# A patch-code convolution block on one core: the softmax numerators of a quad moved one slot behind its logits, with four buffers for the exponentials

## The chip, the cores and the metric

The kernel runs on one core of one Trainium2 chip. The metric is the device time of one execution in microseconds (us). Executions of one kernel on one chip differ by up to 0.6% here, so every kernel is compared through runs of the kernel before on the same chip. A run counts as slow when it is over 1.5% above the fastest of the same kernel.

## The reference, cut to what matters

The block normalises x over groups of channels, then applies two layers. Each layer takes the 3x3 patches p of every channel, weighs that channel's 16 centroids by a softmax of the negative squared distance, and replaces the patch by the weighted centroid before an ordinary multiplication with the weights. A batch norm follows each layer, a ReLU the first, a gate and the residuals the second.

```python
# x: (16, 256, 28, 28) float32; centroids (256, 16, 9); w_sub (256, 9, 256)
def amm_conv3x3(x, centroids, w_sub):
    p = patches(x)                                   # (B, 784, C, 9)
    d = |p|^2 - 2 p.centroids + |centroids|^2        # (B, 784, C, 16)
    attn = softmax(-d)
    lut = einsum('cks,cso->cko', centroids, w_sub)
    return einsum('bnck,cko->bno', attn, lut)
# out = relu(bn(amm1(gn(x)))); out = se(bn(amm2(out))); result = x + relu(out + gn(x))
```

## The kernel before

The work is cut into quads: 4 x 4 tiles of 32x32 on TensorE for one part of the channels and 384 or 400 pixels. A tile of pixels has 8 quads, an image two tiles, a layer 16 quads. The kernel lays one quad of the layer into each *slot*, and lists for a slot, in this order, the logits, the exponentials, some *looks* (128-wide matmuls that add finished quads to the output), the numerators, the turning and scaling of the numerators, and the remaining looks. Engines run their lists in order.

```python
ring = [p_ring.tile([P, 2, 512], F32, name=f"pair{i}") for i in range(3)]   # 3 pairs of PSUM banks
...
def logits(u, rows):                       # TensorE, L563: 16 tiles into two pairs
    ps = [pair(), pair()]
    ...
def b_exp(u):                              # ScalarE, L621: one exponential per pair
    for ps in u.pop("lg"):
        e = epool.tile([P, 2, 400], F32, tag="e", name="e")
        nc.scalar.activation(e[:, :, :n], ps[:, :, :n], AF.Exp, scale=2.0)
def b_num(u):                              # TensorE, L631: numerators and sums, again two pairs
    es = u.pop("e")
    u["nm"] = [pair(), pair()]
    ...
def b_turn(u):                             # VectorE: transposes nt (L643), reciprocal rc (L649)
def c_scale(u):                            # GpSimd: k = nt * rc (L659), tails, range check totals
def c_turn(u):                             # VectorE, a slot later: q = transpose of k (L677)
def c_look(u, o, h):                       # TensorE, L695: acc += ws . q
...
LC = 3                                     # looks of a tile begin 3 slots after its logits
LOGITS, LOAD, MOVE, EXP, LOOK_A, NUM, TURN, SMALL, LOOK_B, MAX, LOOK_C, TURN_BACK, REST = range(13)
...
        def norm(self, b, t):              # group norm of the next image
            self.at(t, REST, gn_stats, b, 0)      # VectorE, needs x
            self.at(t + 1, REST, gn_stats, b, 1)
            self.at(t + 2, SMALL, gn_mean, b)     # TensorE, L423
            self.at(t + 3, SMALL, gn_var, b)      # TensorE, L434
            self.at(t + 4, REST, gn_apply, b, 0)
            self.at(t + 5, REST, gn_apply, b, 1)
...
            plan.at(n0 - 2, REST, load_x, b, x[b])
            plan.norm(b, n0)
```

In the second layer two of each tile's quads also get their maxima ahead of time (another logits block, some VectorE work and a small round trip through DRAM), which makes 576 logits blocks and 512 numerator blocks.

Of the kernel before, what the change touches and what calls it, by code (L numbers as in the profile page):

```python
# [23 lines left out]
NQ = NT // 4  # L24
# [45 lines left out]
def kernel(  # L70
# [328 lines left out]
        nc.vector.tensor_add(wd[l], wd[l], mones_sb[:, l].unsqueeze(1).to_broadcast([P, NT, 32]))  # L399

    tpool = ctx.enter_context(tc.tile_pool(name="tpool", bufs=3))
    epool = ctx.enter_context(tc.tile_pool(name="epool", bufs=2))
    npool = ctx.enter_context(tc.tile_pool(name="npool", bufs=2))
    kpool = ctx.enter_context(tc.tile_pool(name="kpool", bufs=3))
    qpool = ctx.enter_context(tc.tile_pool(name="qpool", bufs=3))
# [314 lines left out]
            )  # L720


    LC = 3
    LOOKS = [(m, o, h) for m in range(NQ) for o in range(2) for h in range(3 if m % 4 == 3 else 2)]

    LOGITS, LOAD, MOVE, EXP, LOOK_A, NUM, TURN, SMALL, LOOK_B, MAX, LOOK_C, TURN_BACK, REST = range(13)

    class Plan:
        def __init__(self, step, lead, lb):
            self.step = step  # L730
            self.lead = lead
            self.lb = lb
            self.ns = len(PXT) * NQ * step
            self.end = self.ns + LC * step
            self.jobs = {}
            self.tiles = []
            self.loads = []

        def at(self, slot, pos, f, *a):
            self.jobs.setdefault((slot, pos), []).append((f, a))  # L740

        def emit(self):

            free = [-99] * len(pts)
            for slot, last, u in sorted(self.loads, key=lambda v: v[:2]):
                tile = free.index(min(free))
                assert free[tile] <= slot
                free[tile] = last
                self.at(slot, LOAD, patches, u, tile)
            for n0, of in self.tiles:  # L750

                slots = [n0 + (LC + q) * self.step for q in range(NQ)]
                more = [2 if (s, MAX) in self.jobs else 0 for s in slots]
                k, room = 0, len(LOOKS) - sum(more)
                for q, s in enumerate(slots):
                    n = (q + 1) * room // NQ - q * room // NQ + more[q]
                    for i, (m, o, h) in enumerate(LOOKS[k : k + n]):
                        self.at(s, LOOK_A if i < n // 2 + n % 2 - more[q] // 2 else LOOK_B if i < n - more[q] else LOOK_C, c_look, of[m], o, h)
                    k += n
            for key in sorted(self.jobs):  # L760
                for f, a in self.jobs[key]:
                    f(*a)

        def stage(self, l, b, pat, s0, maxed):
            at = self.at
            for pi, px in enumerate(PXT):
                n0 = s0 + pi * NQ * self.step
                of = []
                for m in range(NQ):
                    s = n0 + m * self.step  # L770
                    u = {"l": l, "b": b, "pi": pi, "px": px, "pat": pat, "key": (l, b, pi), "m": m, "maxed": m in maxed}
                    of.append(u)
                    if m in maxed:
                        a = s - self.lb
                        self.loads.append((a - self.lead, s, u))
                        at(a, MAX, a_logits, u)
                        at(a, MAX, a_turn, u)
                        at(a + 1, TURN_BACK, a_max, u, 0)
                        at(a + 2, TURN_BACK, a_max, u, 1)
                        at(a + 2, TURN_BACK, m_turn, u)  # L780
                        at(a + 3, MOVE, m_out, u)
                        at(a + 4, MOVE, m_in, u)
                    else:
                        self.loads.append((s - self.lead, s, u))
                    at(s, LOGITS, b_logits, u)
                    at(s, EXP, b_exp, u)
                    at(s, NUM, b_num, u)
                    at(s, TURN, b_turn, u)
                    at(s, TURN, c_scale, u)
                    at(s + 1, TURN_BACK, c_turn, u)  # L790
                self.tiles.append((n0, of))

        def prep(self, l, pat, t):
# [42 lines left out]
    def pat_of(l, b):  # L836
        return d_pat[2 * l + b % 2]
# [17 lines left out]
    plan = Plan(1, 3, 6)  # L855
    for si, (l, b) in enumerate(stages):
        t = si * NS
        plan.stage(l, b, pat_of(l, b), t, () if l == 0 else MAXED)
        if l == 0 and b >= 1:
            n0 = -3 if b == 1 else t - 2 * NS - 3  # L860
            plan.at(n0 - 2, REST, load_x, b, x[b])
            plan.norm(b, n0)
            plan.prep(0, pat_of(0, b), {1: 1, 2: 32, 3: 56}.get(b, t - 2 * NS + 3))
        if l == 1:
            if b in (0, B - 1):
                t0 = t - NS + LC
                plan.prep_near(1, pat_of(1, b), t0, 4, t0 + 4, 8)
            else:
                plan.prep(1, pat_of(1, b), 44 if b == 1 else t - 2 * NS + LC + 1)
            plan.at(t + NS, REST, load_x, b, x[b])  # L870
            plan.close(b, out[b], t + NS + LC, 1 if b < B - 2 else 2)
    for i in range(len(STEPS)):
# [36 lines left out]
    with tc.If(flag > 0):  # L909
        with tc.For_i(0, B) as bi:  # L910
            load_x("g", x[bass.ds(bi, 1)].rearrange("o c n -> (o c) n"))
            plan = Plan(8, 3, 6)
# [84 lines left out]
```

## Time and profile before

| | before |
|---|---|
| median of 3 runs | 2970.67 us |
| span of the profiled run | 2969.2 us |
| granted TensorE clock | 0.989 |
| TensorE / VectorE / ScalarE / GpSimd busy | 97 / 76 / 37 / 60% |

The page follows the chain of work that ended last back from the end, and gives its shares of the span, first by engine and then by line (page of the kernel before):

```profile
PE 79%; DMA 7%; DVE 6%; POOL 4%; issue 2%; ACT 2%; SPq 0%; ACTq 0%; DVEq 0%; POOLq 0%
```

The reader is to see that TensorE is on the path for four fifths of the time, and that some transfers and VectorE work, 13% together, stand on it too. ScalarE, which makes the exponentials, seems to play no part: its short waits, spread over hundreds of slots, show only when a slot is looked at by itself. The lines for that are in the prediction.

### The profile page before, as it was taken

What the parts mean: (1) busy time and instruction counts of PE and PEld (TensorE: products, weight loads), DVE (VectorE), ACT (ScalarE), POOL (GpSimd) and SP (SyncE); (2) the same over time, 40 slices, a digit from 0 to 9 for tenths busy, and PEclk for the clock granted to TensorE, in tenths of its full rate; (3) what the DMA queues carried; (4) which work ended last, traced back from release to release, by engine and by line L of the source; (5) the groups of instructions that cost most, each with busy time, mean ns of one, the idle gap of its engine ahead of it and who ended that gap; (6) DMA issues with size and microseconds to landing.
All of it is one profiled execution on the core that took longest, in us unless ns stands there. A gap on an engine that the chain in (4) does not pass through costs nothing.

```text
span 2969.2 us, 94838 instructions
## 1 busy us (share of the span) xinstructions
PE 2871.6 (97%) x39834; PEld 1145.4 (39%) x39834; DVE 2252.7 (76%) x2760; ACT 1092.7 (37%) x1605; POOL 1768.5 (60%) x2583
## 2 busy tenths in 40 slices
PE   4999999999999999999999999999999999999995
PEld 2433333333333333333333333333333333334332
DVE  3476777787877878787787877878788787878884
ACT  1332343433434343343433434343343434333332
POOL 3474575666656566665656656566665656656553
PEclk8999999999999999999999999999999999999998
DMA  6877777767767676776767667676776767674641
GB/s 185 227 174 170 203 219 195 212 154 213 186 169 197 151 208 174 197 185 154 211 156 207 180 180 188 154 214 156 214 185 163 200 155 206 177 189 106 163 114 56
DMA packets 296773, 530.30 MB, mean 179 GB/s; under 512 B 94240, under 2 KB 251664, under 8 KB 296336
## 3 DMA queue, kind: packets, MB, share of 16 engines
q0 software_dynamic: 51648, 269.78, 34.9%
q1 hardware_dynamic: 242512, 251.70, 32.7%
q8 instruction: 316, 5.18, 0.7%
q10 hardware_dynamic: 2176, 2.65, 0.3%
q14 instruction: 121, 0.99, 0.1%
HBM read 269.96 MB, written 254.05 MB: 176 GB/s over the span
## 4 chain that ended last, share of the span: by engine, by line
PE 79%; DMA 7%; DVE 6%; POOL 4%; issue 2%; ACT 2%; SPq 0%; ACTq 0%; DVEq 0%; POOLq 0%
PE acc L695 47%; PE pair L631 16%; PE pair L563 14%; DMA xt<-in_x 4%; DVE nt L643 2%; POOL k L659 2%; DVE rc L649 1%; DVE gn_st L417 1%; POOL total L671 1%; DMA pt<-pat 1%; ACT e L621 1%; DMA ws<-dws 1%; PE pair L309 0%; PE pair L324 0%; DVE q L677 0%
## 5 line engine op out<-in xcount | busy, mean ns | idle before, releaser
L695 PE MATMUL acc<-q,ws 128*128 128x384 f32 (+1 forms) x4096 | 1641.0, 519 | 9.7 <-ACT y L717 9.7
L659 POOL TENSOR_TENSOR k<-nt,rc 128x832 f32<-128x832 f32 (+1 forms) x512 | 802.3, 1567 | 1132.9 <-DVE rc L649 1120.5
L643 DVE STREAM_TRANSPOSE nt<-pair 128x832 f32<-128x832 f32 (+1 forms) x1024 | 976.3, 992 | 603.5 <-PE pair L631 506.4
L621 ACT ACTIVATE e<-pair 128x800 f32<-128x800 f32 (+1 forms) x1024 | 787.8, 821 | 1358.8 <-PE pair L563 1357.3
L695 PEld LDWEIGHTS acc<-q,ws 128*128 128x128 f32 x4096 | 696.9, 189 | 907.7 <-issue 577.2
L631 PE MATMUL pair<-e,cw 32*32 32x384 f32 (+1 forms) x16384 | 580.3, 502 | 11.9 <-ACT e L621 10.6
L563 PE MATMUL pair<-pt,wd 19*32 19x384 f32 (+2 forms) x18432 | 561.0, 500 | 5.9 <-DMA pt<-pat 3.3
L677 DVE STREAM_TRANSPOSE q<-k 128x832 f32<-128x832 f32 (+1 forms) x512 | 489.1, 955 | 0.8 <-POOL k L659 0.8
L649 DVE RECIPROCAL rc<-nt 128x104 f32<-128x104 f32 (+1 forms) x512 | 398.5, 778 | 17.6
L631 PEld LDWEIGHTS pair<-e,cw 32*32 32x32 f32 x16384 | 167.5, 103 | 349.2 <-ACT e L621 321.4
L563 PEld LDWEIGHTS pair<-pt,wd 19*32 19x32 f32 (+1 forms) x18432 | 138.4, 103 | 340.1 <-issue 265.5
L665 POOL TENSOR_TENSOR tail<-nt,rc 128x104 f32<-128x104 f32 (+1 forms) x512 | 242.4, 473 | 0.0
L695 PE MATMUL acc<-qt,ws 128*128 128x400 f32 (+1 forms) x512 | 218.6, 509 | 0.0
L671 POOL TENSOR_TENSOR total<-total,nt 128x96 f32<-128x96 f32 (+1 forms) x448 | 198.7, 443 | 0.0
L468 POOL DMA_DIRECT2D pat<-side x280 | 186.6, 667 | 1.1 <-DMA pat<-im 0.7
L671 POOL TENSOR_TENSOR total<-total,rc 128x96 f32<-128x96 f32 (+1 forms) x448 | 175.5, 392 | 0.0
L695 PEld LDWEIGHTS acc<-qt,ws 128*128 128x128 f32 x512 | 90.8, 189 | 100.1 <-issue 50.6
L587 DVE TENSOR_REDUCE mx<-z 128x48 f32<-128x768 f32 (+1 forms) x128 | 120.8, 943 | 0.0
L582 DVE STREAM_TRANSPOSE z<-pair 128x768 f32<-128x768 f32 (+1 forms) x128 | 119.2, 969 | 0.0
L468 POOL DMA_DIRECT2D pat<-im x140 | 94.0, 672 | 3.5 <-ACT im L447 3.5
L707 ACT ACTIVATE im<-acc,bnsh,bnsc 128x384 f32<-128x384 f32 (+1 forms) x64 | 43.4, 678 | 139.4 <-PE acc L695 133.4
L717 ACT ACTIVATE y<-acc,bnsh,bnsc 128x384 f32<-128x384 f32 (+1 forms) x64 | 43.4, 679 | 91.7 <-PE acc L695 76.8
(106 smaller groups left out, 753.5 us busy)
## 6 DMA issues: line engine op xcount, KB each, us to landing
pat<-side POOLq DMA_DIRECT2D x232, 588.0 KB, 6.1
pt<-pat SPq DMA_DIRECT2D x1024, 112.5 KB
pt<-pat SPq DMA_DIRECT2D x1024, 108.0 KB
pat<-im POOLq DMA_DIRECT2D x116, 588.0 KB, 5.3
xt<-in_x POOLq DMA_DIRECT2D x32, 784.0 KB, 8.8
out_dram<-y POOLq DMA_DIRECT2D x16, 784.0 KB, 4.0
pat<-side POOLq DMA_DIRECT2D x24, 300.0 KB, 6.1
pat<-side POOLq DMA_DIRECT2D x24, 288.0 KB, 6.0
```

Of the source, the lines that this page charges most:

```text
L468: nc.gpsimd.dma_start(view(pat, (ROWS * p0 + 9 * k + 3 * dx) * HW + px, [[ROWS * HW, m], [HW, 3], [1, n]]), bass.AP(v.tensor, v.offset, [l ...
L563: nc.tensor.matmul(ps[t // 2][c : c + 32, t % 2, :n], lhsT=wd[l][32 * i : 32 * i + rows, 4 * u["m"] + t, :], rhs=u["pt"][32 * i : 32 * i + ...
L587: nc.vector.tensor_reduce(u["mx"][:, 2 * v : 2 * v + 2].rearrange("p t (j b) -> p t b j", j=2)[:, :, :nb], u["z"].pop(0)[:, : 64 * nb].rea ...
L621: nc.scalar.activation(e[:, :, :n], ps[:, :, :n], AF.Exp, scale=2.0)
L631: nc.tensor.matmul(u["nm"][t // 2][32 * i : 32 * i + 32, t % 2, :n], lhsT=cw[l][c : c + 32, 4 * u["m"] + t, :], rhs=es[t // 2][c : c + 32, ...
L643: nc.vector.transpose(nt[:, :nb, 2 * v : 2 * v + 2].rearrange("p b t r -> p t b r"), ps[:, :, : 32 * nb].rearrange("p t (b r) -> p t b r", ...
L649: nc.vector.reciprocal(rc[:, : 8 * nb], u["nt"][:, :, SUM])
L659: nc.gpsimd.tensor_tensor(q[:, :nb].rearrange("p b (a s) -> p (b a) s", s=8), nt[:, :, :8], rc.unsqueeze(2).to_broadcast([P, 8 * nb, 8]), ...
L665: nc.gpsimd.tensor_tensor(tails[key][:, :nb, 8 * (m % 4) : 8 * (m % 4) + 8], nt[:, :, 8].rearrange("p (b a) -> p b a", a=8), rc.rearrange( ...
L671: nc.gpsimd.tensor_add(t[:, : 8 * nb], t[:, : 8 * nb], v)
L677: nc.vector.transpose(q[:, :, : 32 * nb].rearrange("p h (b r) -> p h b r", r=32), u.pop("k")[:, :nb].rearrange("p b (h r) -> p h b r", h=2),)
L695: nc.tensor.matmul(accs[key][:, :n], lhsT=ws[l][:, 2 * m + h if h < 2 else 2 * NQ + m // 4, o * P : (o + 1) * P], rhs=u["q"][h][:, :n], st ...
```

## The change

The intent: the numerators of a quad no longer follow the exponentials of that same quad within the slot. They run one slot later, on exponentials that have long been made, while ScalarE works on the new slot's. For that a pair of exponentials must live a slot longer, hence four buffers; everything behind the numerators moves a slot too, hence LC = 4. The patches of the first and the last image are prepared in three slots instead of four before their first use, to make up for the later outputs.

```diff
-    epool = ctx.enter_context(tc.tile_pool(name="epool", bufs=2))
+    epool = ctx.enter_context(tc.tile_pool(name="epool", bufs=4))
...
-    LC = 3
+    LC = 4
...
-            self.end = self.ns + LC * step
+            self.lc = LC if step == 1 else 3
+            self.end = self.ns + self.lc * step
...
-                slots = [n0 + (LC + q) * self.step for q in range(NQ)]
+                slots = [n0 + (self.lc + q) * self.step for q in range(NQ)]
...
-                    at(s, NUM, b_num, u)
-                    at(s, TURN, b_turn, u)
-                    at(s, TURN, c_scale, u)
-                    at(s + 1, TURN_BACK, c_turn, u)
+                    at(s + 1, NUM, b_num, u)
+                    at(s + 1, TURN, b_turn, u)
+                    at(s + 1, TURN, c_scale, u)
+                    at(s + 2, TURN_BACK, c_turn, u)
...
-                plan.prep_near(1, pat_of(1, b), t0, 4, t0 + 4, 8)
+                plan.prep_near(1, pat_of(1, b), t0, 3, t0 + 3, 8)
```

## The prediction

> **What bounds the kernel now.** I read the page's first part, then the list of waits, then the timeline of a quiet stretch, then the busy time by window. The page's first line and three of its costliest groups:
>
> ```profile
> PE 2871.6 (97%) x39834; PEld 1145.4 (39%) x39834; DVE 2252.7 (76%) x2760; ACT 1092.7 (37%) x1605; POOL 1768.5 (60%) x2583
> ...
> L621 ACT ACTIVATE e<-pair 128x800 f32<-128x800 f32 (+1 forms) x1024 | 787.8, 821 | 1358.8 <-PE pair L563 1357.3
> ...
> L631 PE MATMUL pair<-e,cw 32*32 32x384 f32 (+1 forms) x16384 | 580.3, 502 | 11.9 <-ACT e L621 10.6
> L563 PE MATMUL pair<-pt,wd 19*32 19x384 f32 (+2 forms) x18432 | 561.0, 500 | 5.9 <-DMA pt<-pat 3.3
> ```
>
> TensorE carries the path (79% of the chain that ended last), but its 97% hides gaps, because matmuls overlap. The reader is to see that 16,384 numerator matmuls (L631) are charged 580 us and 18,432 logit matmuls (L563), 12% more of them, only 561 us: the numerators stand still somewhere. The list of waits names the suspects (who waited for whom: total us, times, longest):
>
> ```profile
> PEld pair L631 <- ACT e L621: 321.4, 555, 7.1
> PEld acc L695 <- issue: 627.9, 983, 1.3
> ```
>
> Most of the 321 us is no loss: 0.57 us of idle weight load stands before every small-tile block, logits too, and there it is called "issue". What is lost shows in the timeline of one slot of a quiet stretch (start, us, engine, line, count, idle before):
>
> ```profile
> 1516.05 0.93 PE L563 MATMUL pair<-pt,wd 21*32 21x384 f32 x32
> ...
> 1516.91 1.61 PE L695 MATMUL acc<-q,ws 128*128 128x400 f32 x4
> 1517.09 1.51 ACT L621 ACTIVATE e<-pair 128x768 f32<-128x768 f32 x2 [3.47 <-PE pair L563]
> ...
> 1518.45 1.08 PE L631 MATMUL pair<-e,cw 32*32 32x384 f32 x32
> ...
> 1519.47 1.61 PE L695 MATMUL acc<-q,ws 128*128 128x400 f32 x4
> ...
> 1521.01 0.23 PEld L563 LDWEIGHTS pair<-pt,wd 19*32 19x32 f32 x32 [0.57 <-issue]
> 1521.01 0.93 PE L563 MATMUL pair<-pt,wd 19*32 19x384 f32 x32
> ```
>
> A slot is four blocks: logits, 2 looks (L695), numerators, 2 looks; 4.96 us from 1516.05 to 1521.01. The two blocks of 32 small matmuls have the same shape but one takes 1.08 and the other 0.93. The two exponentials end at 1518.60; the numerators begin at 1518.45 with the first pair's, and the second pair's must wait for the second exponential. In the single records of this block the last start lies 0.60 us after the first; in the logits 0.45. So this slot loses 0.15 us, between two halves of one block, and nothing before the block.
>
> **Size of that loss over the whole trace.** For each of the 512 numerator blocks I took the distance from first to last start and subtracted 0.46 us (the undisturbed distance is 0.45 to 0.46). 138 blocks lose nothing (mostly slots with three looks ahead of the numerators, whose two extra 0.34 us matmuls cover the exponentials), 321 lose 0.10 to 0.30, and 42 lose 0.60 to 0.70 (the exponentials stand behind copies and evacuations on ScalarE). Sum: **95.1 us**: 3.8 before 135 us, 2.4 to 230, 1.6 to 282, 2.7 to 380, 80.5 in 380 to 2790, 4.2 after. A second loss is the whole block starting late for the first exponential: 8.3 us in 31 blocks, and once 6.5 us at 78 us.
>
> **What the Trainium skill says.** "Trainium Kernel Development and Optimization", Performance Expectations, says that matmul busy time is a bad metric because matmuls are pipelined; the trace agrees (97% busy beside 95 us of stalls). "TensorE: Matmul & The Clock Gate", Part 3, The mechanism, says matmuls start and end in strict program order; so the waiting half-block holds the looks behind it, and the trace agrees: L695 at 1519.47 follows the last numerator by the same 0.41 us as after logits. "TensorEngine Tiling (Array Packing)", Key Properties: "Mode switching requires drain"; the 627.9 us of "issue" before 128-wide weight loads, about 0.65 us each, look like it. "PSUM — Partial Sum Buffer", its part on bank collisions, asks that a bank be guarded until its reader is done; the ring of three PSUM pairs does that, and it makes the first rival below.
>
> **The change part by part.**
> - *Numerators one slot later.* The two program-order listings of TensorE show the same four blocks a slot, in the same places: logits, looks, numerators, looks. Two looks still lie between logits and numerators, so "next to" removes no change of tile mode: 0 us. What moves is which exponentials the block needs: those of a slot ago, about 4 us old. The listing shows its first half waiting for VectorE alone.
> - *Four exponential buffers.* A pair of exponentials now lives a slot longer; with four, the write of the next finds its buffer freed by the numerators of the slot before. No wait, no cost.
> - *The ring.* The numerators' second half writes the pair from which the first exponential of the same slot reads. In the quiet slot that one (half of 1.51 us from 1517.09) ends near 1517.9, and the second half may start at 1518.5: 0.6 us to spare. So the 95.1 us go, but the late starts (8.3 and 6.5 us) largely stay, now on the second half.
> - *LC 3 to 4.* One more slot of looks at the end, with as much less at the start: I count +2 us, since the start is held by transfers. The early preparation for the first and last image is squeezed from four slots to three, and the first second-layer stage already waits for transfers (11.5 us of stalls in logits blocks between 230 and 282 us): +4 there, +2 for the last image, both my choice.
>
> Gross gain: 80.5 + 2.4 + 2.7 + 4.2 = 89.8, plus 1.5 of the first 3.8, about 91 us; nothing from 230 to 282.
>
> What is given back in each image, over some 15 images:
>
> ```profile
> core 0: us, PE busy (x) PEld busy (x) DVE busy (x) ACT busy (x) POOL busy (x), PEclk, DMA share, GB/s
> ...
> 1466.00:1486.00 20.00, 20.00 (x290) 7.91 (x290) 18.81 (x21) 9.19 (x13) 16.60 (x22) 1.00 0.77 194
> ```
>
> Here VectorE is busy 18.81 of 20 us (the y additions of 1.19 us join the usual 3.85 us a slot), so of the 0.73 us of stalls in these slots about 0.4 will come back as waits for VectorE: 6 us. And where the next image's x lands (a transfer of about 10 us that holds VectorE's statistics, after which logits lose 0.5 us at 1597), an earlier arrival only waits longer: about 0.3 us an image, 4 us.
>
> Sum: 91 - 2 - 4 - 2 - 6 - 4 = 73 us; 2970.7 - 73 is about **2897 us**, 2.5% less.
>
> **The rivals.**
> - *The ring's wait takes the place of the removed one*: then 2950 to 2970. For it: the PSUM ring is unchanged. Against: 0.6 us to spare in common slots; only the 31 late blocks lack it.
> - *VectorE becomes the bound.* Its first numerator transpose must end before the second half of the next logits. Measured from nt's end to that start, common slots have 0.56 us to spare now, 0.29 where there is no stall already, so removing 0.15 to 0.27 leaves about 0.3. For it: in 104 of the 436 slots between 380 and 2790 us VectorE had under 0.1 us idle ahead of that transpose; these hold 17.8 us of the stalls. If all that were lost, and as much again around it: 2930.
> - *Tile modes*: if the blocks became neighbours, two of four mode changes a slot would go, some hundred us more. The listing speaks against it.
> - *Transfers bind*: 68% of the transfer engines' time is used; 0.90 in the stretch from 1586 to 1602. A few us, counted above.
>
> **Range and chances.** Keeping 91 us and giving back half of what I charged makes about 2882; losing the 17.8 us and twice the start costs makes about 2920. Range 2874 to 2922. The 2% line is at 2911.3, or 59 us of gain: faster 0.82, within 2% 0.17, slower 0.01.
>
> **What will show it.** In a quiet slot the numerator block takes 0.93 us like the logits and the slot is 4.80 us; the excess sum falls from 95 to under 15 us; the row of L631's loads waiting for the exponential shrinks or turns into "issue"; the count of matmuls and the mode changes stay; VectorE rises to about 78%. Wrong would be: halves of L631 waiting for the new slot's exponentials (first rival), logits blocks split by waits for the transpose nt with VectorE without idle (second), or stalls between 230 and 290 us grown by over 10 us.

## The result

The changed kernel took 2901.87 us (median of 3 runs, 2893.94 to 2902.28), against 2970.67 us before: ratio 0.9758, with a 95% interval from 0.9732 to 0.9785. A ratio here is the mean time of one kernel's fast runs over that of the other's of the same rounds, so not quite the ratio of the medians quoted. It is 68.8 us less.

The same two parts of the page as in the prediction, now of the changed kernel (engines' busy time; then the two matmul groups, logits first):

```profile
PE 2786.8 (96%) x39834; PEld 1103.5 (38%) x39834; DVE 2249.5 (78%) x2760; ACT 1096.2 (38%) x1605; POOL 1771.1 (61%) x2583
...
L563 PE MATMUL pair<-pt,wd 19*32 19x384 f32 (+2 forms) x18432 | 567.8, 501 | 19.8 <-DVE nt L643 11.1
L631 PE MATMUL pair<-e,cw 32*32 32x384 f32 (+1 forms) x16384 | 486.3, 501 | 5.5 <-ACT e L621 5.5
```

The numerators' busy time fell from 580.3 to 486.3 us for the same number of instructions of the same length: the holes inside their blocks are gone. The logits rose from 561.0 to 567.8, and there is now something to read behind their bar: 19.8 us of idle time ahead of them, 11.1 of it for the transpose nt. The list of waits of the changed kernel (who waited for whom: total us, times, longest):

```profile
PEld pair L631 <- issue: 145.2, 257, 1.1
PEld pair L631 <- DVE q L677: 117.8, 212, 0.6
...
PE pair L434 <- POOL gn_dv L428: 17.3, 14, 1.3
...
PE pair L563 <- DVE nt L643: 11.1, 14, 1.7
PEld pair L631 <- ACT e L621: 10.1, 8, 4.5
```

The row of 321.4 us that named the exponentials is down to 10.1. What is left ahead of the numerators' weight loads is the 0.57 us that stand before every block of small tiles, which the list puts down to "issue" or to whatever VectorE finished last. Two rows grew: the variance matmul L434 waited 4.2 us before and 17.3 now, in 14 images, and the logits waited for nt (1.6 us before, 11.1 now). A slot of the changed kernel in the timeline:

```profile
1483.70 0.93 PE L563 MATMUL pair<-pt,wd 21*32 21x384 f32 x32
...
1484.56 1.61 PE L695 MATMUL acc<-q,ws 128*128 128x400 f32 x4
1484.74 1.51 ACT L621 ACTIVATE e<-pair 128x768 f32<-128x768 f32 x2 [3.32 <-PE pair L563]
...
1486.10 0.95 PE L631 MATMUL pair<-e,cw 32*32 32x400 f32 x32
...
1486.98 1.61 PE L695 MATMUL acc<-q,ws 128*128 128x400 f32 x4
...
1488.52 0.93 PE L563 MATMUL pair<-pt,wd 19*32 19x384 f32 x32
```

The numerators (here of the tile before, 400 pixels wide) take 0.95 us and run through, although the second exponential beside them ends only at 1486.25. Over all slots with two looks before and two behind, the median length fell from 5.00 us (334 slots) to 4.80 us (335 slots).

**Where the time went**, from the starts of all matmuls in the two traces. "Inside" is from the first to the last start of a block; "ahead" is from the last start of the block before to its first.

| block | inside | ahead |
|---|---|---|
| numerators L631 | -88.9 us | -14.1 us |
| logits L563 | +14.4 | +5.6 |
| variance L434 | 0 | +13.1 |
| mean L423 | 0 | -6.8 |
| looks L695 | +4.4 | -4.5 |
| sorting of the weights at the start (L324) | +2.5 | +6.2 |

The excess of the numerator blocks, defined as in the prediction, fell from 95.1 to 8.8 us. Of the 8.8, 7.7 are two blocks at 69 and 78 us. The logits' excess rose from 23 to 37 us over the whole run, and from 8.0 to 23.2 in the stretch of the middle images.

**Where it was given back.** One of twelve such places in the middle of the changed kernel. The next image's x is asked for, and ten microseconds later VectorE's statistics L417, the transposes nt and the logits follow each other:

```profile
1207.16 0.74 POOL L147 DMA_DIRECT2D xt<-in_x  x1
...
1214.88 0.95 PE L631 MATMUL pair<-e,cw 32*32 32x400 f32 x32
...
1217.30 0.90 PE L563 MATMUL pair<-pt,wd 19*32 19x400 f32 x16
1217.64 1.04 DVE L417 BATCH_NORM_STATS2 gn_st<-xt 128x6 f32<-128x392 f32 x2 [2.33 <-DMA xt<-in_x]
...
1218.84 1.94 DVE L643 STREAM_TRANSPOSE nt<-pair 128x832 f32<-128x832 f32 x2
1219.90 0.18 PEld L563 LDWEIGHTS pair<-pt,wd 19*32 19x32 f32 x16 [2.42 <-DVE nt L643]
```

VectorE had been free since 1215.3 and stood 2.33 us at the head of its list for x. The transposes behind it, whose data were ready, came late; the second half of the next logits needs the PSUM pair that the first transpose frees, and stood 2.42 us. The same place in the kernel before lost 0.41 us:

```profile
1233.09 0.74 POOL L147 DMA_DIRECT2D xt<-in_x  x1
...
1242.40 0.95 PE L631 MATMUL pair<-e,cw 32*32 32x400 f32 x32
...
1243.04 1.04 DVE L417 BATCH_NORM_STATS2 gn_st<-xt 128x6 f32<-128x392 f32 x2 [1.57 <-DMA xt<-in_x]
...
1244.24 1.93 DVE L643 STREAM_TRANSPOSE nt<-pair 128x832 f32<-128x832 f32 x2
...
1245.29 0.18 PEld L563 LDWEIGHTS pair<-pt,wd 19*32 19x32 f32 x16 [0.28 <-DVE nt L643]
```

What changed is the time that x is given. From the request for x to the start of the numerators whose transpose it delays there were 9.31 us, and now there are 7.73 (medians of the twelve images); from the request to the statistics it takes 10.10 and 9.78 us on the mean. The three slots that end with these numerators took 16.73 us and take 15.17 in nine of the twelve images: of the 1.56 us, 0.84 are removed holes and about 0.67 two look instructions that now lie elsewhere (26 instead of 28). VectorE's own idle time ahead of the statistics fell, from 23.0 to 18.9 us over the run, so it does not measure the loss; the wait that it causes on TensorE does.

### The profile page after: what moved, and what is told of

Same layout as the page of the kernel before. It is cut to its first block, busy times and chain, and to the rows that moved or that the text cites. A ratio compares the mean times of both kernels' runs of the same rounds, so it can differ in the third digit from the quotient of the medians.

```text
span 2900.4 us, 94662 instructions
## 1 busy us (share of the span) xinstructions
PE 2786.8 (96%) x39834; PEld 1103.5 (38%) x39834; DVE 2249.5 (78%) x2760; ACT 1096.2 (38%) x1605; POOL 1771.1 (61%) x2583
## 4 chain that ended last, share of the span: by engine, by line
PE 80%; DMA 7%; POOL 5%; DVE 4%; issue 3%; ACT 0%; SPq 0%; DVEq 0%; POOLq 0%; ACTq 0%
PE acc L695 50%; PE pair L563 15%; PE pair L631 13%; DMA xt<-in_x 4%; POOL k L659 2%; DVE nt L643 2%; DMA pt<-pat 1%; POOL total L671 1%; POOL pat L468 1%; DVE rc L649 1%; POOL tail L665 1%; PE pair L324 1%; DVE gn_st L417 1%; DMA pt<-dm 1%; DMA dm<-mt 0%
## 5 line engine op out<-in xcount | busy, mean ns | idle before, releaser
L695 PE MATMUL acc<-q,ws 128*128 128x384 f32 (+1 forms) x4096 | 1645.8, 520 | 5.1 <-ACT y L717 5.1
L695 PEld LDWEIGHTS acc<-q,ws 128*128 128x128 f32 x4096 | 698.8, 190 | 904.4 <-issue 579.0
L563 PE MATMUL pair<-pt,wd 19*32 19x384 f32 (+2 forms) x18432 | 567.8, 501 | 19.8 <-DVE nt L643 11.1
L631 PE MATMUL pair<-e,cw 32*32 32x384 f32 (+1 forms) x16384 | 486.3, 501 | 5.5 <-ACT e L621 5.5
L563 PEld LDWEIGHTS pair<-pt,wd 19*32 19x32 f32 (+1 forms) x18432 | 140.2, 103 | 357.8 <-issue 270.3
L665 POOL TENSOR_TENSOR tail<-nt,rc 128x104 f32<-128x104 f32 (+1 forms) x512 | 236.3, 462 | 0.0
L631 PEld LDWEIGHTS pair<-e,cw 32*32 32x32 f32 x16384 | 119.9, 103 | 294.1 <-issue 145.2
L695 PE MATMUL acc<-qt,ws 128*128 128x400 f32 (+1 forms) x512 | 220.6, 513 | 0.0
L695 PEld LDWEIGHTS acc<-qt,ws 128*128 128x128 f32 x512 | 91.7, 191 | 100.7 <-issue 52.1
L533 POOL TENSOR_TENSOR y<-y,xt 128x392 f32<-128x392 f32 x64 | 69.2, 1084 | 10.4 <-ACT y L529 10.4
```

The lines of the kernel that those rows point to most:

```text
L563: nc.tensor.matmul(ps[t // 2][c : c + 32, t % 2, :n], lhsT=wd[l][32 * i : 32 * i + rows, 4 * u["m"] + t, :], rhs=u["pt"][32 * i : 32 * i + ...
L631: nc.tensor.matmul(u["nm"][t // 2][32 * i : 32 * i + 32, t % 2, :n], lhsT=cw[l][c : c + 32, 4 * u["m"] + t, :], rhs=es[t // 2][c : c + 32, ...
L665: nc.gpsimd.tensor_tensor(tails[key][:, :nb, 8 * (m % 4) : 8 * (m % 4) + 8], nt[:, :, 8].rearrange("p (b a) -> p b a", a=8), rc.rearrange( ...
L695: nc.tensor.matmul(accs[key][:, :n], lhsT=ws[l][:, 2 * m + h if h < 2 else 2 * NQ + m // 4, o * P : (o + 1) * P], rhs=u["q"][h][:, :n], st ...
```

## The experiments

The theory after the result: (1) the gain is the numerators' wait for the exponentials, most of it the half-block's for the second one; (2) about 25 us were given back where the next image is normalised, because the slots in which x has to arrive got shorter while the transfer of x and the chain from it to the variance did not; (3) the three PSUM pairs, and not the exponentials, are what binds the order inside a slot now. The rivals: the buffers made the gain; VectorE is simply full; the distance between the blocks and the changes of tile mode decide.

### Four buffers alone

```diff
# on the kernel before
-    epool = ctx.enter_context(tc.tile_pool(name="epool", bufs=2))
+    epool = ctx.enter_context(tc.tile_pool(name="epool", bufs=4))
```

> The kernel before with four exponential buffers and nothing else. If the gain comes from the numerators needing exponentials of a slot ago, the buffers alone change nothing: 2970 us within 4, and the excess of the numerator blocks (last start less first start less 0.46 us, summed) stays at 95 us. If the buffers themselves were what held the exponentials back, most of the gain would show: about 2905 us.

Measured: 2972.57 us, ratio 1.0001 (0.9985 to 1.0016). Numerators' excess in the middle images (between 380 and 2730 us): 79.3 us, against 78.8 in the kernel before. The buffers alone do nothing; they are what lets the numerators move. The opposite part, the move with two or three buffers, could not be tried: the exponentials of the new slot are written into the program ahead of the numerators that free their buffers, and the program does not build.

### Three looks before the numerators, in the old slots

```diff
# on the kernel before
-  LOOK_A if i < n // 2 + n % 2 - more[q] // 2 else ...
+  LOOK_A if i < n // 2 + 1 - more[q] // 2 else ...
```

> The kernel before, no slot moved, but three looks ahead of the numerators and one behind where it was two and two: the exponentials get 0.67 us more. Theory: the numerators' excess falls from 95 us to under 25 as in the change, but the transpose nt, which must end before the second half of the next logits and had about 0.35 us to spare without the stall, is now about 0.3 us late in each such slot: logits' excess above 90 us, 2980 to 3040 us. Rival (only the wait for the exponentials matters): 2890 to 2915 us, as the change.

Measured: 3019.85 us, ratio 1.0182 (1.0158 to 1.0206). The numerators' excess fell to 8.9 us, as in the change; the logits' rose to 147.1, in 289 of 576 blocks by 0.25 to 0.45 us each. Two lines of its timeline, and the weight load between the halves:

```profile
1547.32 1.83 DVE L643 STREAM_TRANSPOSE nt<-pair 128x768 f32<-128x768 f32 x2
...
1547.98 1.24 PE L563 MATMUL pair<-pt,wd 19*32 19x384 f32 x32
1548.34 0.18 PEld L563 LDWEIGHTS pair<-pt,wd 19*32 19x32 f32 x16 [0.19 <-DVE nt L643]
```

The first of the two transposes ends at 1548.2, and only then may the second half of the logits start (1548.3). So the wait for the exponentials can be removed without moving a slot, but it comes back larger on the other side of the numerators. The move takes it away without shortening either distance. This also bears out the number that the prediction worked with, some 0.3 us to spare for the transpose where there is no stall: two look instructions more put the numerators 0.67 us later, and the next logits then waited 0.3 to 0.4.

### The blocks side by side

```diff
# on the changed kernel
-  LOGITS, LOAD, MOVE, EXP, LOOK_A, NUM, TURN, SMALL, ...
+  LOGITS, LOAD, MOVE, EXP, NUM, TURN, LOOK_A, SMALL, ...
```

> The changed kernel with the numerators placed directly behind the logits on TensorE, all looks of a slot behind both: what the few words on the change could also mean. Two of the four changes of tile mode in a slot go, which by the spacing of starts is worth about 0.35 us a slot; but the second half of the numerators writes the PSUM pair that the new slot's first exponential has still to read, which ends about 1.9 us after the logits began, where the half could start at 0.7. Theory (the ring binds): a hole of about 1.15 us inside each numerator block, slot 5.6 us, 3200 to 3330 us in all. Rival (mode changes matter most): 2700 to 2760 us.

Measured: 3255.58 us (one run, state unknown). The numerators' excess is 619.2 us, 1.21 us a block, and 511 of 512 blocks have it; a slot with eight look instructions takes 5.57 us. Its timeline:

```profile
1607.15 0.95 PE L563 MATMUL pair<-pt,wd 19*32 19x400 f32 x32
...
1607.85 2.17 PE L631 MATMUL pair<-e,cw 32*32 32x400 f32 x32
...
1608.22 1.57 ACT L621 ACTIVATE e<-pair 128x800 f32<-128x800 f32 x2 [3.56 <-PE pair L563]
...
1609.11 0.18 PEld L631 LDWEIGHTS pair<-e,cw 32*32 32x32 f32 x16 [0.84 <-ACT e L621]
```

The numerators' exponentials are a slot old here, and yet the second half waits until 1609.11 for an exponential: not to read it, but for the one that began at 1608.22 to have read the pair that this half overwrites. This is the ring's wait. In the changed kernel the looks stand between and cover it, except in the two blocks at 69 and 78 us, where there are no looks yet.

### x asked for two slots earlier, and the same on the kernel before

```diff
# on the changed kernel, and in the control on the kernel before
-            plan.at(n0 - 2, REST, load_x, b, x[b])
+            plan.at(n0 - (2 if b == 1 else 4), REST, load_x, b, x[b])
```

> The changed kernel with the next image's x asked for two slots earlier. Theory: what was given back is the statistics waiting for x at the head of VectorE's queue, with the transpose nt and so the second half of the next logits behind them; then the logits' excess between 380 and 2730 us falls from 23.2 us to under 8, and the time by 12 to 18 us, to 2884 to 2890 us. Rival, VectorE is simply full there: the excess stays above 15 us and the time within 4 us of 2902.

> The kernel before with x two slots earlier, as a control. There the logits' excess in the same stretch is 8.0 us, so theory: 3 to 7 us gained, 2964 to 2968 us. If it gained 12 us or more, the wait for x would not be something that the change made larger.

Measured on the changed kernel: 2905.88 us, ratio 0.9772 (0.9755 to 0.9789): no gain, so the number missed. The logits' excess did fall, from 23.2 to 4.4 us, but 18.9 us of new waits ahead of logits blocks took its place, 2.6 to 5.1 us each in five images. One of them:

```profile
1374.11 0.74 POOL L147 DMA_DIRECT2D xt<-in_x  x1
...
1374.67 2.50 SPq L608 DMA_DIRECT2D pt<-dm  x2
...
1384.48 1.65 PE L563 MATMUL pair<-pt,wd 21*32 21x400 f32 x32 [4.46 <-DMA pt<-dm]
```

The earlier x is asked for 0.56 us before the maxima of a quad (pt<-dm), and these arrive late; four of the five waits end with the maxima, one with patches. That x beside them is the reason is read from the trace and was not tried by itself. TensorE idles 4.46 us, and the looks that follow start 0.67 us apart instead of 0.34, at a granted clock of 0.50 from 1384.4 to 1388.0. That agrees with "TensorE: Matmul & The Clock Gate", Part 1: an idle stretch of about 3.4 us halves the clock for a while. So the chain was right and the remedy wrong. On the kernel before: 2968.92 us, ratio 0.9986 (0.9969 to 1.0003), excess from 8.5 (in the four-buffer run beside it) to 0.5 us, new waits 3.3 us: a few us at most, as expected.

### The variance one slot later

```diff
# on the changed kernel, from the third image on (late = 1)
-            self.at(t + 3, SMALL, gn_var, b)
-            self.at(t + 4, REST, gn_apply, b, 0)
-            self.at(t + 5, REST, gn_apply, b, 1)
+            self.at(t + 3 + late, SMALL, gn_var, b)
+            self.at(t + 4 + late, REST, gn_apply, b, 0)
+            self.at(t + 5 + late, REST, gn_apply, b, 1)
```

> The changed kernel with the variance matmul (L434) and the normalisation one slot later, from the third image on. The distance from the matmul before to L434 rose from 11.7 to 24.7 us over 16 images. Theory: L434 stands at the head of TensorE's queue for GpSimd's two small operations, which stand behind a quad's scaling; a slot later they are done, the distance falls to about 9 us and the time by 10 to 14 us, to 2888 to 2892. Rival: the wait is only a piece of the wait for x and turns up elsewhere: within 4 us of 2902.

Measured: 2892.14 us, ratio 0.9728 (0.9711 to 0.9746), some 9 us by the ratios (0.9728 against 0.9758). The distance ahead of L434 fell from 24.7 to 7.1 us; the logits' excess stayed (26.3 us in the middle images). The wait for the variance can be removed by itself; what that brings in time is less sure, since the intervals of the two ratios overlap (a second measurement of the change, below, would make it 17 us).

### The statistics one slot later, x where it was

```diff
# on the changed kernel, from the third image on
-            plan.norm(b, n0)
+            plan.norm(b, n0 + int(b > 1))
```

> The changed kernel with the normalisation's four steps one slot later (from the third image on) and the load of x where it was, so that x has three slots in place of two and no transfer moves. Asking for x earlier had removed the logits' excess (23.2 to 4.4 us between 380 and 2730 us) but put 18.9 us of waits for patches and maxima in its place. Theory: it is the wait of the statistics, and it can go without a new one: excess under 8 us, waits ahead of logits blocks under 4 us, 14 to 20 us gained, 2882 to 2888 us. Rival, VectorE is too full there: within 4 us of 2902.

Measured: 2874.24 us, ratio 0.9677 (0.9658 to 0.9695). The logits' excess in the middle images fell from 23.2 to 2.9 us, the waits ahead of logits blocks stayed at 1.7. It gained more than expected (24 us by the ratios, 32 by the second measurement of the change, against 14 to 20): with earlier statistics relative to the rest, the mean and the variance are less late as well, and the distance ahead of L434 fell to 12.1 us.

### Both delays, the control, and the change again on one chip

```diff
# on the changed kernel, and in the control on the kernel before
-            plan.norm(b, n0)
-            plan.prep(0, pat_of(0, b), {1: 1, 2: 32, 3: 56}.get(b, t - 2 * NS + 3))
+            plan.norm(b, n0 + int(b > 1), int(b > 1))        # late = 1 as above
+            plan.prep(0, pat_of(0, b), {1: 1, 2: 32, 3: 56}.get(b, t - 2 * NS + 4))
```

> Both delays: statistics and mean one slot later, variance and normalisation two, the patches of the next image one. Theory: the two waits are separate and add up: about 10 us for the variance (6 us to 11 us in the run of that alone) and 16 for the statistics, 2872 to 2880 us. If they are one and the same wait, no better than the better of the two: 2885 to 2892.

Measured: 2870.35 us, ratio 0.9669 (0.9654 to 0.9684). The distance ahead of L434 is 7.1 us and the logits' excess 2.3. The time is as expected, but its interval overlaps that of the statistics alone (0.9677), so these runs do not show that the two delays add up: in good part they are one chain.

> A control: the kernel before (numerators in the slot of their logits, two exponential buffers) with the same delays of the statistics, the variance and the next image's patches. Theory: the wait of the half-block for the exponentials is still there (about 95 us of excess in the numerators), and the delays take only the 8 us of excess in the logits and a few us more: 2955 to 2964 us. If the delays were a gain of their own, not a repair of what the change gave back, this would gain the 30 us that they gained on the changed kernel: about 2940.

> The changed kernel again, on the same chip as the two beside it: ratio to the kernel before 0.9758 within 0.002, so 2893 to 2905 us.

> The changed kernel with both delays again, on the same chip: ratio 0.9669 within 0.002, 2865 to 2878 us. The step from the control to this run is then what the move itself is worth where nothing is given back: by the numerators' excess about 95 us, less 2 to 7 us at start and end: 83 to 95 us.

The three shared a chip:

| kernel | us | ratio to before (95%) | numerators' excess | logits' excess, whole run |
|---|---|---|---|---|
| before | 2972.17 | 1 | 95.1 (its first trace) | 22.7 (its first trace) |
| control: old slots, both delays | 2955.51 | 0.9945 (0.9931 to 0.9958) | 96.6 | 14.1 |
| the change | 2910.41 | 0.9784 (0.9765 to 0.9804) | 8.7 | 39.2 |
| the change with both delays | 2869.10 | 0.9656 (0.9643 to 0.9670) | 14.1 | 13.2 |

The change alone came out at 0.9784, a little over the band written down for it (0.9758 within 0.002) but within the interval of the first measurement (0.9732 to 0.9785); the first value lies just under this interval (0.9765 to 0.9804). So the change is known to some 0.3% only. The delays are worth 17 us in the old slots and 41 us on the change by the medians (16 and 38 by the ratios); so some 22 to 25 us of them repair what the change gave back, and the rest was there to be had before. From control to last row the move is worth 86.4 us, in the band of 83 to 95 written down. Between these two traces the numerators' excess fell by 82.5 us, and the distance ahead of numerator blocks by another 11.0; some of that is lost again elsewhere. The last row, 3.4% under the kernel before, is the fastest version and correct.

## Why the prediction was right

- **The loss it started from.** Holes of 95.1 us inside the numerator blocks, for the second exponential. Shown: the excess fell to 8.8 us, a quiet slot to 4.80 us as written, and on one chip, with the give-back out of the way, the move gained 86.4 us. The move was always run with LC = 4, and in the first and last image with the shorter preparation; neither was tried alone.
- **No mode change removed.** Shown: looks, numerators and logits keep their order in the slot, and putting the blocks really side by side costs 350 us.
- **The ring has 0.6 us to spare.** Right for the common slots. It also said that the late starts (8.3 us, and 6.5 once) would largely stay on the second half. The 6.5 did, in the two blocks at 69 and 78 us (7.7 us of excess). The 8.3 did not: numerator blocks that start within 0.15 us of the end of the slot's first exponential, or before it, fell from 46 to 19. With LC = 4 the evacuations, a slot later, meet other work on ScalarE; that this is the reason was read from the traces and not tried by itself.
- **VectorE full, 6 us.** Too much. With the wait for x removed, the logits' excess in all middle images is 2.3 us, in a kernel that runs 32 us faster still.
- **The wait for x, 4 us.** This is the term that was most mis-sized. Between the 50th and the 540th logits block the chain from x took 24 us: 17 ahead of and inside logits, 13 ahead of the variance, less 6 ahead of the mean. The prediction had seen the place but counted about 0.3 us an image for the logits, where x got some 1.6 us less time, and nothing for the variance. The whole chain (x, statistics, mean, two GpSimd steps, variance) did not get shorter with the slots, and TensorE stands in order at two ends of it.
- **Start and end.** The first second-layer stage did not get 4 us worse: the changed kernel was 2.3 us ahead at its 28th logits block (231.8 us in the kernel before), 2.1 at the 36th (283.9) and 3.8 at the 51st (354.9). The last 35 blocks gained 8.8 us, 4.6 of it because TensorE waited 5.1 instead of 9.7 us for the buffer of the last output; why was not tried. The end itself cost 4.9 us instead of the 2 charged: 46 instead of 36 look instructions stand behind the last logits block, about 3.4 us at 0.336 each.

So the sum was right (73 us against 69) because the large term had been measured, and because errors of the small ones nearly cancelled, which is luck. The chain from x was charged some 20 us too little (4 against 24), and the end about 3. Too much was charged, or too little gained, for VectorE, for the late starts, for the first second-layer stage and for the last image, together some 20 us. One sum in the range was wrong as well: 91 us kept and half of the 18 us charged make 2889 us, not 2882. The division among the terms is an account by reading the two traces; only the first term, and that of the chain, were tried by themselves.

## What to carry to other kernels

A block whose halves need different producers is best measured by the spread of its instructions' starts against a twin block that does not wait; here 0.15 us in each of hundreds of slots made 95 us, while the engines' busy shares and the chain showed nothing of it. Moving the consumer by a slot removed the wait here; reordering inside the slot only handed it on to the next buffer's release, and cost 50 us. And when slots get shorter, look for the chains whose length is counted in slots but made of transfers and small steps: give each of them one slot more at the same time, by starting its consumer later rather than its transfer earlier.

## What the Trainium skill lacked or had wrong

- "TensorEngine Tiling (Array Packing)", Key Properties, says that changing the tile mode drains TensorE, but gives no price. Here, logits and numerators with four look instructions between them: 0.42 us from the last small start to the first look, 1.11 for the looks, 0.43 to the next small block (medians). Side by side: 0.24 between the two blocks, and the four looks cost 4 x 0.336 elsewhere. A pair of mode changes is therefore worth about 0.38 us here.
- No page looked up gives a price for a ring of PSUM buffers that is too short for the order of the blocks: side by side, with three pairs for two-pair blocks, neighbours cost 1.21 us a slot (619 us), though every input was ready.
- None of the pages looked up warns that one in-order engine passes a late transfer on to another: at one place 2.33 us of VectorE's wait for x became 2.42 us of TensorE's, for a PSUM pair that had nothing to do with x.
